# The first stage of a routed cross-attention kernel: biases and condition in one transpose, router's and anchor's products beside the scores, scaling on ScalarE, one difference on GpSimd

## The chip, the cores and the metric

The kernel runs on one core of one Trainium2 chip. The metric is the device time of one execution in microseconds. The profile is taken by the hardware profiler from one more execution of the same program.

## The reference

All arrays are fp32. B = 8 batches, T = 512 tokens, H = 256, RH = 512, E = 3 experts, 64 context rows.

```python
nx = layer_norm(x, ln_gamma, ln_beta)
q, k, v = nx @ Wq, ctx @ Wk, ctx @ Wv
weights = softmax(einsum('bth,bph->btp', q, k) * H ** -0.5)
evidence = einsum('btp,bph->bth', weights, v)
anchor = broadcast(cond[:, None, :])
combined = concat([nx, evidence, anchor], -1)            # 3 H wide
router_probs = softmax(combined @ router_W + router_b)
h = silu(einsum('btc,ecr->bter', combined, e_w1) + e_b1)
expert_out = einsum('bter,erh->bteh', h, e_w2) + e_b2
routed = sum(expert_out * router_probs[..., None], -2)
g = sigmoid(silu(combined @ gate_w1 + gate_b1) @ gate_w2 + gate_b2)
out = x + g * (routed @ out_w + out_b)
```

## The kernel before

The batches are worked in four pairs j = 0 to 3. Features lie on the partitions, tokens along the free axis, so most products are 128 x 128 weights against 512 tokens. Keys are folded into one matrix (`join_keys`, then `project(wkqT, ctxT, keep_m, "m")` gives `mr`), and values are multiplied with the weights beforehand (`value_weights` gives `vw`), so that evidence enters the hidden layers as a product of `vw` with the turned softmax weights `wT`. The products of x with the weights are done in seven instead of eight, Winograd's way: `combine_x` makes differences T (`t1`, `t2`, `t4`) of the four blocks of the scaled x and `t3` in place of a block of `nxT`, and `combine_weights` makes sums `ws` of the weights. `nx_product(j, n, which)` is one of the seven; product 7 reads `t3`, product 3 the block beside it.

The change lies in the work ahead of pair 0 and in the head of its gate layer:

- Loads. SyncE (queue SP) and ScalarE's queue load context, x and the large weights. GpSimd's queue loads the small ones: the biases and the layer norm's vectors into the tile `rows` (28 rows of 128, line 204), the condition into `cond_sb` (8 rows of 256, line 206), `router_W` (line 208) and the router's bias (lines 211, 212). This part of the program is put in order by a scheduler from the dependencies.
- Behind `with tc.manual_schedule(engines=None)` (line 1419) the order on each engine is the order of the program text.
- `small_transposes` (L301) turns `rows` into `cols` (biases, gamma and beta by partition) and the two halves of the condition into `condT`. Its PSUM banks come from `either`, others from `misc`; both hand out banks in turn.
- `statistics`, `deviation`, `normalize` make the normalized rows of x on VectorE with a square root on ScalarE; `transpose_x` (L580) turns them on TensorE, and `scale_x` (L570) scales them out of PSUM, even blocks on VectorE, odd ones on ScalarE.
- `keep_m` (L362) copies the first column of each batch out of PSUM (`m0`) and subtracts it from the others, both on VectorE.
- `router_anchor` (L378) multiplies the condition and beta with the router's columns; `store_router_anchor`, `spread_router_bias` carry its result through DRAM to all partitions on GpSimd's queue.
- `anchor_rows(g)` (L436) multiplies the condition with the anchor part of expert g's or the gate's weights (g = E), 32 columns of weights at a time, four beside each other.
- `scores` (L648), `sum_weights`, `softmax`, `turn_weights` are the attention of pair 0 up to `wT`.
- `gate_layer` (L921) runs the seven products of the gate, with steps of the setup put between by name (`steps.get("gate")`), and ends in `evidence`, which reads `wT` and `vw`.

The order before, as the program text gives it: `small_transposes`, `transpose_x(0)`, `m`, `router_anchor`, `transpose_x(1)`, the gate's `vw`, `scores`, expert 0's `vw`, `anchor_rows(E)`, `anchor_rows(0)`, then the gate layer.

Of the kernel before, what the change touches and what calls it, by code (L numbers as in the profile page):

```python
# [9 lines left out]
AF = mybir.ActivationFunctionType  # L10
# [6 lines left out]
def kernel(  # L17
# [90 lines left out]
    def misc(name):  # L108
        spare.append(spare.pop(0))
        return bank(spare[-1], name)  # L110
# [55 lines left out]
    def by_k(flat, n):  # L166
# [9 lines left out]
    scr = scratch(0, 0, "scr_wa0")  # L176
    wa = {0: by_k(scr[:, :HK], RH), E: by_k(scr[:, HK : HK + KH * H], H)}
    scr = scratch(1, 0, "scr_small")
    zeros, rows, cond_sb = scr[:, :P], scr[:, P : 2 * P], scr[:B, 2 * P : 2 * P + H]
    NL = 2 * P + H  # L180
    rw, rw2, m0, rw_all, gamma_all = (
        scr[:, NL : NL + 3 * KH * E].rearrange("p (k e) -> p k e", e=E),
        scr[:, NL + P : NL + P + KH * TB].rearrange("p (k e) -> p k e", e=TB),
        scr[:, NL + 2 * P : NL + 2 * P + B],
        scr[:, NL + 4 * P : NL + 4 * P + H * E].rearrange("p (d e) -> p d e", e=E),
        scr[:, NL + 4 * P + H * E : NL + 4 * P + H * E + H],
    )
    nc.vector.memset(zeros, 0.0)
    nc.vector.memset(eps_t, LN_EPS)
    nc.vector.memset(warm_t, 1.0)  # L190

    NR = NE + 5 * KH + E * KH
    rows = rows[:NR, :]
    r = 0
    for src, n in (
        (e_b1.rearrange("e (c p) -> (e c) p", p=P), NE),
# [6 lines left out]
    ):  # L203
        nc.gpsimd.dma_start(rows[r : r + n, :], src)
        r += n
    nc.gpsimd.dma_start(cond_sb, cond)
    anchor = slice(2 * H, 3 * H)
    nc.gpsimd.dma_start(rw, rows_of(router_W))
    rb_c = const.tile([ED, 2], F32, tag="rb_c", name="rb_c")
# [77 lines left out]
    def either(name):  # L287
        turn[0] += 1
        return bank((1, 2, 0, 3)[turn[0] % 4], name)
# [10 lines left out]

    def small_transposes():  # L301
        pt = either("pt_rows")
        nc.tensor.transpose(pt[:, :NR], rows, ident[:NR, :NR])
        nc.vector.tensor_copy(cols, pt[:, :NR])
        nc.gpsimd.tensor_copy(b2T[:, :, :E], b2_c.rearrange("p e k -> p k e"))
        pt = either("pt_cond")
        for k in range(KH):
            nc.tensor.transpose(
                pt[:, k * B : (k + 1) * B], cond_sb[:, k * P : (k + 1) * P], ident[:B, :B]
            )  # L310
        nc.vector.tensor_copy(
            condT[:, :, :B], pt[:, : KH * B].rearrange("p (k b) -> p k b", b=B)
        )

    def context_transposes():
# [45 lines left out]

    def keep_m(m, ps):  # L362
        ps = ps.rearrange("p (b c) -> p b c", c=CT)
        nc.vector.tensor_copy(m0, ps[:, :, 0])
        nc.vector.tensor_tensor(
            mr[:, m, :, 1:], ps[:, :, 1:], m0.unsqueeze(2).to_broadcast([P, B, CT - 1]), ALU.subtract
        )


# [6 lines left out]
    rbd = dram.tile([2, NP, ED], F32, tag="rbd", name="rbd")  # L376

    def router_anchor():  # L378
        ps = misc("ps_rb")
        for k in range(KH):  # L380
            nc.tensor.matmul(
                ps[:ED, :B], rwd[:, 2 * KH + k, :], condT[:, k, :B], start=(k == 0), stop=False
            )
        for k in range(KH):

            nc.tensor.matmul(
                ps[:ED, :B], rw2[:, k, :ED], beta_c[:, k : k + 1].to_broadcast([P, B]),
                start=False, stop=(k == KH - 1),
            )
        dst = rrow.rearrange("e (i j) -> e j i", i=2)  # L390
        src = ps[:ED, :B].rearrange("e (j i) -> e j i", i=2)
        nc.scalar.activation(dst, src, AF.Identity, bias=rb_c[:, 0:1])
# [43 lines left out]
    def anchor_rows(g):  # L436


        n = RC if g < E else KH
        ps = misc(f"ps_ar_{g}")[:, : n * QB]  # L440
        for k in range(KH):
            w = wa[g][:, k, :].rearrange("p (c i f) -> p i c f", i=P // QB, f=QB)
            for i in range(P // QB):
                nc.tensor.matmul(  # L444
                    ps[i * QB : (i + 1) * QB, :].rearrange("p (c f) -> p c f", f=QB),
                    condT[:, k, :], w[:, i, :, :], start=(k == 0), stop=(k == KH - 1),
                )
        ar[g] = setup.tile([P, n * QB], F32, tag="ar", name=f"ar_{g}")
        nc.vector.transpose(ar[g], ps)
# [120 lines left out]
    def scale_x(dst, k, src, vector):  # L570
        if vector:
            nc.vector.tensor_scalar(
                dst, src, gamma_c[:, k : k + 1], beta_c[:, k : k + 1], ALU.mult, ALU.add
            )
        else:
            nc.scalar.activation(
                dst, src, AF.Identity, bias=beta_c[:, k : k + 1], scale=gamma_c[:, k : k + 1]
            )

    def transpose_x(b):  # L580
        S["nxT", b] = npool.tile([P, KH, T], F32, tag="nxT", name=f"nxT_{b}")
        for k in range(KH):
            pt = misc(f"pt_x_{b}_{k}")
            for t in range(NT):
                nc.tensor.transpose(  # L585
                    pt[:, t * P : (t + 1) * P], S["xn", b][:, t, k * P : (k + 1) * P], ident
                )
            scale_x(S["nxT", b][:, k, :], k, pt, k % 2 == 0)

    def logits(j):  # L590

# [278 lines left out]
    def keep_part(n, i, d, part):  # L870
        nc.scalar.copy(chunk(n, i, d), part)  # L871
# [49 lines left out]
    def gate_layer(j, steps):  # L921
        n = 0
        for i in range(2):
            for k in range(KH):
                S["hg", i, k] = hpool.tile([P, T], F32, tag=f"hg{i}{k}", name=f"hg_{2 * j + i}_{k}")
        U[n], Z[n], Y[n] = (bank(i, f"ps_{u}_{j}_{n}") for i, u in ((0, "u"), (2, "z"), (3, "y")))
        nx_product(j, n, 1, True)
        keep_part(n, 0, 0, U[n])
        if j == 0:
            anchor_columns(E)  # L930
            anchor_columns(0)
        spares(7, 5)
        nx_product(j, n, 5, True)
        keep_part(n, 1, 1, Z[n])
        nx_product(j, n, 2, True)
        nx_product(j, n, 6)
        keep_part(n, 1, 0, U[n])
        nx_product(j, n, 3)
        for step in steps.get("gate", ()):
            step()  # L940
        nx_product(j, n, 7)
        add(n, 1, 1, U[n])
        for step in steps.get("gate end", ()):
            step()
        if j:
            return
        W = bank(1, f"ps_w_{j}")
        fresh(j, 0)
        evidence(j, [(m, True) for m in PAIRS[0]], W=W)

        add(n, 0, 0, Y[n])
        add(n, 1, 0, Z[n])
        add(n, 1, 1, W)
        silu(j, n, 0, 0)
# [464 lines left out]
    with tc.manual_schedule(engines=None):  # L1419
# [30 lines left out]
        deviation(0, 1)  # L1450
        load_router_column()
        normalize(1)
        load_table(AF.Exp)
        project(wkqT, ctxT, keep_m, "m")
        router_anchor()
        transpose_x(1)
        value_weights(0, E)
        store_router_rows(0)
        store_router_anchor()
        combine_weights(E)  # L1460
        combine_x(0, nc.vector, (0, 1))
        scores(0)
        router_column()
        spread_router_bias()
        combine_weights(0)
        spread_router_rows(0)
        value_weights(0, 0, nc.scalar.copy, False)
        anchor_rows(E)
        anchor_rows(0)
        sum_weights(0)  # L1470
        softmax(0)
        value_differences(0, 0)
        combine_x(0, nc.vector, (2,))
        turn_weights(0)
        late_scratch()
        load_anchor(1)
# [5 lines left out]
        for j in range(NP):  # L1482
# [5 lines left out]
                where.setdefault(n, []).append(lambda: step(*args))  # L1488

            if j == 0:  # L1490
                put(within, "gate", value_weights, 0, 1, nc.scalar.copy, False)
                put(within, "gate", load_table, AF.Silu)
                put(within, (0, "S"), combine_x, 0, nc.vector, (3,))
                put(within, (0, "S"), value_differences, 0, 1)
# [105 lines left out]
```

## Time and profile before

| | |
|---|---|
| median of 3 runs | 459.14 us (458.96 to 460.01) |
| the profiled execution | 458.79 us, of which 456.80 us are the span of the core |
| granted TensorE clock | 1.00 |
| TensorE matmul busy | 451.4 us, 99% of the span |
| VectorE, ScalarE, GpSimd busy | 365.1 us (80%), 213.9 us (47%), 100.2 us (22%) |
| evidence of the first gate begins on TensorE at | 31.33 us |

The span runs from the first to the last instruction of the program; the profiled execution's own time is 2.0 us longer. Times within the span are given in microseconds from its start. Busy time of TensorE is modelled from pipelined matmuls, so gaps between them are read from the start times. PEld is TensorE's weight load, a q behind an engine's name its sequencer.

### The profile page before, as it was taken

The numbers are of one execution on the slowest core, as the hardware profiler recorded it, in microseconds if no ns is written. First come the engines' busy times: TensorE is split into PE (matmuls) and PEld (weight loads), VectorE is DVE, ScalarE is ACT, GpSimd is POOL, SyncE is SP. The second block draws the span as 40 slices with busy tenths as digits, with TensorE's granted clock in tenths as the row PEclk, the third lists the DMA queues.
The fourth block names the chain that finished last, engine by engine and source line by source line (L and its number), as shares of the span: only waits on it lengthen the run. The fifth ranks groups of instructions, "written<-read, shape, count | busy, mean of one in ns | idle before, by whom it ended". The sixth has DMA issues, their size and how long they took to land.

```text
span 456.8 us, 5304 instructions
## 1 busy us (share of the span) xinstructions
PE 451.4 (99%) x1713; PEld 211.5 (46%) x1713; DVE 365.1 (80%) x683; ACT 213.9 (47%) x370; POOL 100.2 (22%) x149
## 2 busy tenths in 40 slices
PE   8999999999999999999999999999999999999997
PEld 6544555444444444444444444444444444444445
DVE  2888979969699999479689999578869846677983
ACT  3445683655221585467220576468220456558000
POOL 6447715001072300001062400001044300000010
PEclk9999999999999999999999999999999999999999
DMA  8975587302011387203011368103011390000014
GB/s 279 371 155 133 97 239 121 93 0 46 7 23 23 56 241 130 83 0 48 6 23 23 48 222 129 20 0 48 6 23 23 50 219 12 0 0 1 0 15 77
DMA packets 119402, 35.30 MB, mean 77 GB/s; under 512 B 106044, under 2 KB 116336, under 8 KB 118864
## 3 DMA queue, kind: packets, MB, share of 16 engines
q1 hardware_dynamic: 115312, 27.02, 29.1%
q0 software_dynamic: 2176, 7.17, 4.8%
q10 hardware_dynamic: 1888, 0.79, 0.6%
q8 instruction: 13, 0.21, 0.2%
q14 instruction: 13, 0.11, 0.1%
HBM read 27.56 MB, written 7.39 MB: 77 GB/s over the span
## 4 chain that ended last, share of the span: by engine, by line
PE 98%; DMA 1%; DVE 0%; SPq 0%; issue 0%
PE ps_u L804 45%; PE ps_z L804 20%; PE ps_y L804 14%; PE ps_vw L777 5%; PE ps_gu L804 3%; PE ps_w2o L505 2%; PE ps_s L655 2%; PE ps_gz L804 2%; PE ps_tokens L804 1%; DMA scr_ctx<-in_ctx_dram 1%; PE ps_v L343 1%; PE ps_m L343 1%; PE ps_gy L804 1%; PE ps_ar L444 0%; PE ps_kq L356 0%; PE pt_x L585 0%
## 5 line engine op out<-in xcount | busy, mean ns | idle before, releaser
L804 PE MATMUL ps_u<-nxT,w 64*128 64x512 f32 (+1 forms) x184 | 86.9, 592 | 0.0
L919 DVE TENSOR_TENSOR h<-h,pb 128x512 f32<-128x512 f32 x96 | 63.4, 697 | 14.9 <-ACT h L862 12.2
L804 PE MATMUL ps_u<-h,w2o 128*128 128x512 f32 x144 | 64.2, 595 | 0.0
L862 ACT ACTIVATE h<-h,abias 128x512 f32<-128x512 f32 x72 | 49.3, 718 | 24.4 <-DVE h L868 24.2
L804 PE MATMUL ps_z<-wT,vw 64*128 64x512 f32 x104 | 51.6, 593 | 0.0
L1324 POOL TENSOR_TENSOR yb<-yb,xb 128x512 f32<-128x512 f32 x14 | 17.7, 1266 | 148.7 <-DVE yb L1323 131.3
L804 PE MATMUL ps_z<-T,ws 64*128 64x512 f32 (+1 forms) x92 | 46.4, 590 | 0.0
L804 PE MATMUL ps_z<-nxT,ws 64*128 64x512 f32 (+1 forms) x92 | 45.9, 590 | 0.0
L804 PE MATMUL ps_y<-nxT,w 64*128 64x512 f32 (+1 forms) x92 | 45.5, 590 | 0.0
L804 PEld LDWEIGHTS ps_u<-nxT,w 64*128 64x128 f32 (+1 forms) x184 | 33.1, 188 | 26.7 <-issue 24.2
L804 PE MATMUL ps_u<-T,ws 64*128 64x512 f32 (+1 forms) x92 | 42.8, 590 | 0.0
L804 PE MATMUL ps_z<-h,w2s 128*128 128x512 f32 x96 | 42.5, 592 | 0.0
L804 PE MATMUL ps_u<-T,w 64*128 64x512 f32 (+1 forms) x98 | 42.4, 590 | 0.0
L804 PEld LDWEIGHTS ps_u<-h,w2o 128*128 128x128 f32 x144 | 27.0, 190 | 32.6 <-issue 30.4
L871 ACT COPY h<-ps_u 128x512 f32<-128x512 f32 x48 | 27.9, 581 | 24.3 <-PE ps_u L804 22.3
L419 POOL DMA_DIRECT2D vrd<-vw x8 | 5.0, 628 | 134.6 <-ACT vw L784 134.6
L1291 DVE TENSOR_TENSOR h<-h,h 128x1024 f32<-128x1024 f32 x24 | 34.3, 1485 | 0.0
L804 PEld LDWEIGHTS ps_z<-h,w2s 128*128 128x128 f32 x96 | 18.2, 190 | 23.0 <-issue 22.3
L804 PE MATMUL ps_y<-wT,vw 64*128 64x512 f32 x56 | 28.0, 596 | 0.0
L804 PE MATMUL ps_u<-wT,vw 64*128 64x512 f32 x56 | 27.9, 595 | 0.0
L777 PE MATMUL ps_vw<-w,vT 128*128 128x512 f32 (+1 forms) x64 | 26.9, 542 | 0.0
L868 DVE TENSOR_TENSOR h<-h,ps_u 128x512 f32<-128x512 f32 x24 | 16.1, 684 | 11.2 <-PE ps_u L804 11.1
(229 smaller groups left out, 811.9 us busy)
## 6 DMA issues: line engine op xcount, KB each, us to landing
pb<-pd POOLq DMA_DIRECT2D x4, 1536.0 KB, 6.5
xb<-in_x_dram SPq DMA_DIRECT2D x64, 64.0 KB, 2.5
out_dram<-yb SPq DMA_DIRECT2D x56, 64.0 KB, 2.0
w<-in_L_xcond_e_w_dram SPq DMA_DIRECT2D x6, 512.0 KB, 10.5
x<-in_x_dram SPq DMA_DIRECT2D x24, 128.0 KB, 3.1
xd<-x SPq DMA_DIRECT2D x24, 128.0 KB, 2.4
xg<-xd SPq DMA_DIRECT2D x48, 64.0 KB, 2.4
scr_wa<-in_L_xcond_e_w_dram SPq DMA_DIRECT2D x3, 512.0 KB, 16.7
```

The lines of the kernel that those rows point to most:

```text
L343: nc.tensor.matmul(ps, w_sb[:, k, m * P : (m + 1) * P], src[:, k, :], start=(k == 0), stop=(k == KH - 1))
L419: nc.gpsimd.dma_start(S["vrd", j][i].rearrange("e c -> c e"), S["vw", j][row_half(i), R0:])
L505: nc.tensor.matmul(ps[:, d * H : (d + 1) * H], w2T[:, k, (i + d) * P : (i + d + 1) * P], ow_sb[:, k, :], start=(k == 0), stop=(k == KH - 1),)
L655: nc.tensor.matmul(ps[side(i, h), g * NH : (g + 1) * NH], mr[:, k, 2 * j + i, g * TB : (g + 1) * TB], S["nxT", 2 * j + i][:, k, h * NH : ( ...
L777: nc.tensor.matmul(ps, vT[:, k, j * 2 * CT : (j + 1) * 2 * CT], w1[:, KH + k, n0:n1], start=(k == 0), stop=(k == KH - 1),)
L804: return nc.tensor.matmul(ps, lhsT, rhs, start=start, stop=True, skip_group_check=not start)
L862: nc.scalar.activation(h, h if src is None else src, AF.Silu, bias=abias[:, c, 2 * j + i : 2 * j + i + 1])
L868: nc.vector.tensor_tensor(h, h, part, ALU.add)
L871: nc.scalar.copy(chunk(n, i, d), part)
L919: nc.vector.tensor_tensor(h, h, S["pb", j][:, i, :, 2 * q // RC, :], ALU.mult)
L1291: nc.vector.tensor_tensor(d, p, m, ALU.subtract)
L1324: nc.gpsimd.tensor_tensor(yb, yb, S["xb", 2 * j + row][:, i, :], ALU.add)
```

## The change

It does five things. (1) The condition is loaded as two DMAs of 8 rows of 128 behind the 28 rows of `rows`, all 128 rows of that tile are set to zero first, and one 128 x 128 transpose gives both `cols` and `condT`. (2) `router_anchor` and `anchor_rows(E)` move to between the gate's `vw` and `scores`, `anchor_rows(0)` directly behind `scores`, and the loading of the table for Exp behind them. (3) For the first x both blocks are scaled by ScalarE; the `m0` copies go to ScalarE, into a place of their own for each half. (4) `t3` of pair 0 is made by GpSimd directly behind its sums of the gate's weights. (5) Expert 1's `vw` is computed before the gate's product 3 and no longer behind it.

```diff
-    zeros, rows, cond_sb = scr[:, :P], scr[:, P : 2 * P], scr[:B, 2 * P : 2 * P + H]
+    zeros, rows = scr[:, :P], scr[:, P : 2 * P]
...
-        scr[:, NL + 2 * P : NL + 2 * P + B],
+        scr[:, NL + 2 * P : NL + 2 * P + KH * B],
...
-    nc.vector.memset(zeros, 0.0)
+    nc.vector.memset(scr[:, : 2 * P], 0.0)
...
-    rows = rows[:NR, :]
...
-    nc.gpsimd.dma_start(cond_sb, cond)
+    for k in range(KH):
+        nc.gpsimd.dma_start(rows[r : r + B, :], cond[:, k * P : (k + 1) * P])
+        r += B
...
         pt = either("pt_rows")
-        nc.tensor.transpose(pt[:, :NR], rows, ident[:NR, :NR])
+        nc.tensor.transpose(pt[:, :P], rows, ident)
         nc.vector.tensor_copy(cols, pt[:, :NR])
         nc.gpsimd.tensor_copy(b2T[:, :, :E], b2_c.rearrange("p e k -> p k e"))
-        pt = either("pt_cond")
-        for k in range(KH):
-            nc.tensor.transpose(
-                pt[:, k * B : (k + 1) * B], cond_sb[:, k * P : (k + 1) * P], ident[:B, :B]
-            )
         nc.vector.tensor_copy(
-            condT[:, :, :B], pt[:, : KH * B].rearrange("p (k b) -> p k b", b=B)
+            condT[:, :, :B], pt[:, NR : NR + KH * B].rearrange("p (k b) -> p k b", b=B)
         )
...
-        nc.vector.tensor_copy(m0, ps[:, :, 0])
+        first = m0[:, m * B : (m + 1) * B]
+        nc.scalar.copy(first, ps[:, :, 0])
         nc.vector.tensor_tensor(
-            mr[:, m, :, 1:], ps[:, :, 1:], m0.unsqueeze(2).to_broadcast([P, B, CT - 1]), ALU.subtract
+            mr[:, m, :, 1:], ps[:, :, 1:], first.unsqueeze(2).to_broadcast([P, B, CT - 1]), ALU.subtract
         )
...
-        ps = misc("ps_rb")
+        ps = either("ps_rb")
...
-        ps = misc(f"ps_ar_{g}")[:, : n * QB]
+        ps = (either if g == E else misc)(f"ps_ar_{g}")[:, : n * QB]
...
-            scale_x(S["nxT", b][:, k, :], k, pt, k % 2 == 0)
+            scale_x(S["nxT", b][:, k, :], k, pt, b > k)
...
         keep_part(n, 1, 0, U[n])
+        for step in steps.get("gate early", ()):
+            step()
         nx_product(j, n, 3)
...
         normalize(1)
-        load_table(AF.Exp)
         project(wkqT, ctxT, keep_m, "m")
-        router_anchor()
         transpose_x(1)
         value_weights(0, E)
+        router_anchor()
+        anchor_rows(E)
         store_router_rows(0)
         store_router_anchor()
         combine_weights(E)
+        load_table(AF.Exp)
         combine_x(0, nc.vector, (0, 1))
         scores(0)
+        anchor_rows(0)
+        combine_x(0, nc.gpsimd, (2,))
         router_column()
         spread_router_bias()
         combine_weights(0)
         spread_router_rows(0)
         value_weights(0, 0, nc.scalar.copy, False)
-        anchor_rows(E)
-        anchor_rows(0)
         sum_weights(0)
         softmax(0)
         value_differences(0, 0)
-        combine_x(0, nc.vector, (2,))
         turn_weights(0)
...
-                put(within, "gate", value_weights, 0, 1, nc.scalar.copy, False)
+                put(within, "gate early", value_weights, 0, 1, nc.scalar.copy, False)
```

## The prediction

> **What bounds the kernel now.** I read the chain of waits on the page first, then TensorE's timeline over the stage that the change touches, then GpSimd's timeline, the DMA issues and the sequencer's rows.
>
> ```profile
> PE 98%; DMA 1%; DVE 0%; SPq 0%; issue 0%
> ```
>
> TensorE is 98% of the chain that ended last, at a granted clock of 1.00 in every stage. So only three things can move the time: TensorE work, the gaps between its instructions, and what it waits for. The change acts before 32 us; behind that, the instruction streams of all engines keep their order. The stage, on TensorE:
>
> ```profile
> 12.54 0.24 PE L303 MATMUL pt_rows<-ident,scr_small 28*128 28x28 f32 x1
> 12.62 0.26 PE L308 MATMUL pt_cond<-ident,scr_small 8*128 8x8 f32 x2
> 12.81 1.09 PE L585 MATMUL pt_x<-ident,x 128*128 128x128 f32 x8
> 13.74 3.60 PE L343 MATMUL ps_m<-scr_ctx,scr_k 128*128 128x512 f32 x8
> 17.27 0.25 PE L381 MATMUL ps_rb<-condT,rwd 128*2 128x8 f32 x4
> 17.37 0.24 PE L386 MATMUL ps_rb<-cols,scr_small 128*2 128x8 f32 x4
> 17.55 1.09 PE L585 MATMUL pt_x<-ident,x 128*128 128x128 f32 x8
> 18.48 1.03 PE L777 MATMUL ps_vw<-w,vT 128*128 128x258 f32 x4
> 19.69 1.93 PE L655 MATMUL ps_s<-nxT,mr 128*32 128x256 f32 x32 [0.18 <-DVE nxT L572]
> 21.55 1.98 PE L777 MATMUL ps_vw<-w,vT 128*128 128x512 f32 x4
> 23.47 0.87 PE L444 MATMUL ps_ar<-scr_wa,condT 128*32 128x64 f32 x32
> 24.27 0.70 PE L804 MATMUL ps_u<-nxT,w 128*128 128x512 f32 x1
> ```
>
> First column start, second busy time. Only the scores show a wait (0.18 us, for VectorE's scaled x). Taken instruction by instruction the starts show small gaps too. A 512-column fp32 step is 0.429, but 0.52 before the router's products (16.75 to 17.27) and before the anchor's (22.95 to 23.47): about 0.09 at each change from full to narrow weights. Changing back costs 0.10 before and 0.10 behind the first full matmul (24.27 to 24.80 is 0.53).
>
> GpSimd's queue, which loads the rows that L303 and L308 transpose:
>
> ```profile
> 1.29 0.66 POOL L204 DMA_DIRECT2D scr_small<-in_L_xcond_e_b_dram  x1 [0.35 <-issue]
> ...
> 2.28 0.52 POOL L204 DMA_DIRECT2D scr_small<-in_L_xcond_gate_b_dram  x1
> ...
> 5.27 0.51 POOL L206 DMA_DIRECT2D scr_small<-in_cond_dram  x1
> 6.33 0.88 POOL L208 DMA_DIRECT2D scr_small<-in_L_xcond_router_W_dram  x1 [0.55 <-DMA scr_small<-in_L_xcond_e_b_dram]
> ```
>
> Eight DMAs go out back to back; the ninth (router_W) waits until the first has landed, because GpSimd's DMAs use eight completion semaphores in turn. Issue to landing:
>
> ```profile
> scr_small<-in_L_xcond_e_b_dram POOLq DMA_DIRECT2D x1, 6.0 KB, 4.8
> ...
> scr_small<-in_cond_dram POOLq DMA_DIRECT2D x1, 8.0 KB, 6.0
> scr_small<-in_L_xcond_router_W_dram POOLq DMA_DIRECT2D x1, 9.0 KB, 6.4
> ```
>
> So cond lands at 5.27 + 6.0 = 11.3, and TensorE's sequencer passes that wait just then:
>
> ```profile
> L308 PEldq EVENT_SEMAPHORE  x1: 51/51/51, 11.3 to 11.3; - x1
> ```
>
> TensorE comes to these rows at 12.54. The cover is 1.2 us.
>
> **TensorE's work, part by part.** Four stretches, before against after.
> - *Rows to ps_m.* 12.54 to 13.74 is 1.20. The two cond transposes go; the rows' one grows from 28 to 128 columns, one transpose step of 0.11. With eight transposes of x at 0.93 that is about 1.05: gain 0.15.
> - *ps_m to ps_vw.* 13.74 to 18.48 is 4.74. Without the eight router products (0.025 each) and their two changes it is 8 x 0.429 + 8 x 0.109 = 4.31: gain 0.43.
> - *ps_vw to the scores.* 18.48 to 19.69 is 1.21: 0.87 of work, 0.34 of change and wait. Now the router's products (0.09 + 0.20) and the gate's anchor rows (23.47 to 23.72, 0.25, with about 0.15 for changes) stand there: 0.87 + 0.69 = 1.56, loss 0.35. The wait has to be gone for this; see VectorE below.
> - *Scores to the gate's first product.* 19.69 to 24.27 is 4.58. Now scores, expert 0's anchor rows and vw follow each other: 1.75 + 0.35 + 0.20 (change) + 1.82 = 4.12: gain 0.46; the gate's first matmul needs no change behind it: gain 0.10.
>
> Sum: 0.15 + 0.43 - 0.35 + 0.46 + 0.10 = 0.8 us of gain, if nothing is late. The earlier ps_vw for expert 1 only changes place with the gate's product 3: nothing.
>
> **The other engines.** Both scalings of the first x go to ScalarE (0.78 each), also the two m0 copies (0.16 on VectorE); ScalarE sat idle 0.72 and 0.92 around there, and its second Sqrt comes some 0.7 later. VectorE normalizes x_1 accordingly later, still 0.2 before TensorE turns it; then two mr subtractions (0.68) and one scaling (0.80) end 0.1 to 0.4 before the scores, by whose place the moved products have added 0.5 of cover. Were that cover gone it would cost the old 0.2. The softmax chain on VectorE, scores to wT, was 10.65 long (19.69 to 30.34) against 11.64 until TensorE's evidence at 31.33. It loses 0.69 (the third difference) and TensorE loses 0.5 there, so 1.1 of slack stays. The third difference on GpSimd takes 1.26 to 2.25 (the same lines in later pairs); it starts after combine_weights(E), about 3.5 behind the scores' start, and product 7 needs it at 10.3: hidden by 4.5 at least. The router's bias load, gg and combine_weights(0) behind it on GpSimd move by at most that; the first was waiting 5.7 for its DMA, and ws of expert 0, ready at 35.2, is read at 38.5.
>
> What GpSimd's subtraction does to VectorE, this trace bounds by its own neighbours:
>
> ```profile
> L646 DVE TENSOR_TENSOR T<-nxT,T x2: 692/824/955, 20.5 to 34.8; 128x512 f32<-128x512 f32 x2
> ```
>
> The 955 ns one ran beside GpSimd subtractions: 0.26 more, so 0 to 0.5 over two instructions, inside the slack; I take none. The Trainium skill, "SBUF — State Buffer", section "Who interferes with whom", speaks against the move: a VectorE instruction with two SBUF inputs and a GpSimd one that reads block each other for a whole instruction. By that rule wT could come 2.25 later, 1.1 beyond the slack, and the sum would be 1.1 worse; the row shows a quarter of a microsecond.
>
> **The queue.** This is the dear part. The zeroing of VectorE now covers the rows, so the rows' DMAs depend on it and the scheduler puts router_W ahead of all of them; cond becomes two DMAs. In GpSimd's built order cond's halves are the ninth and tenth: the first waits for router_W's landing, the second for e_b1's. And TensorE's one transpose now waits for all nine row DMAs.
> - router_W issues at 1.29 and takes 0.88, or 0.15 more as the first (the first of before took 0.66 against 0.50). With the 0.33 that the mask took, e_b1 issues at 2.50 to 2.66.
> - It lands 4.8 to 5.0 later (its own row, and gate_b's, which was second), at 7.3 to 7.6; GpSimd goes on 0.26 after a landing (6.07 to 6.33). So cond's second half issues at 7.6 to 7.9.
> - Issue to landing at that hour: 5.7 for the two rb_c loads issued at 7.43 and 8.10, 6.0 for cond. Far ends: 4.8 and 6.4. So it lands at 13.3 to 13.9; with the far ends at 12.4 to 14.3. I take 13.6, with rb_c's and cond's rows, the nearest in time and in shape.
>
> TensorE then begins the rows at 13.64 in place of 12.54: 1.1 of new wait. Everything behind it shifts alike, since its followers (columns, scaling, ps_m) are fed by it.
>
> A page prices this otherwise: the Trainium skill, "DMA: Bandwidth & Descriptors", section "Anatomy of one DMA — SWDGE (gpsimd) path", fits about 2.0 us and bytes over 436e3. By it the half would land at about 9.8, no wait would arise and the change would gain 0.9; the rows of this trace are 4.8 to 6.4, and they decide.
>
> **Sum.** 1.1 of wait less 0.8 is +0.3 us. The profiled execution took 458.79 (span 456.80, 2.0 around it), which gives 459.1; the median of the three runs lies 0.35 above the profiled one, so 459.14 + 0.3, rounded up for the untested followers of the wait, is 459.5.
>
> **Rivals.**
> 1. *The rows arrive in time* (the wait does not arise): needs the half landed before 12.5, 4.7 after issue. For it: e_b1 took 4.8. Against it: the ten later loads of that queue took 4.9 to 6.4. The gain is then the 0.8 and a further 0.1 (no idle before the transposes): 458.2. At partial waits it lies between.
> 2. *Slower: router_W's 768 pieces of 12 bytes land late and hold the whole chain.* Place: the first half of cond, which waits for router_W's semaphore. At its own 6.4 it lands at 7.7 and the halves issue at 8.0 and 8.5; landing 5.9 later is 14.4, TensorE waits 1.9, net +1.1, and with the 6.4 row for the half as well +1.6: 460.2 to 460.7. It decides from a landing of router_W after 7.4, since before that e_b1's is later. For it: the longest row. Against it: in that row the queue already had seven others ahead; as the first it has none, and the 4.8 of the first fits better.
> 3. *GpSimd's subtraction holds VectorE* past its slack: +0.3 to +1.1, 459.8 to 460.6, from 1.1 of delay on. The 0.26 row speaks against it.
> 4. *It does not do what it says*: if the scores still wait for VectorE, the loss is 0.2, inside the forecast.
>
> **How the numbers follow.** Forecast (landing 13.1 to 14.1) 0.60; rows in time, wholly or half, 0.14; late router_W 0.21; GpSimd against VectorE 0.05. A measurement of this kernel tells about 0.2%, 0.92 us, from no change: below 458.2 is faster, above 460.06 slower. The forecast's own range, -0.2 to +0.8 beside 459.14, lies within. Rival 1 sits on the lower bound: 0.06 faster, 0.08 same. Rivals 2 and 3 are beyond the upper one in most of their reach: 0.22, with 0.06 more from the forecast's tail, 0.28. That leaves 0.66. The range 458.5 to 460.4 leaves out about 0.08 below and 0.12 above.
>
> **What would show it.** Right: router_W first in GpSimd's timeline, cond's second issue at 7.6 to 7.9 with a wait ahead of it, pt_rows at 13.3 to 13.9 with idle "<- DMA scr_small<-in_cond", pt_rows to scores 6.9 long (7.15 before), scores to ps_u 4.1, no wait of TensorE for nxT or wT. Wrong: pt_rows at 12.5; a wait at the scores, at product 7 or at the evidence; any difference behind 32 us.

## The result

The changed kernel took 459.85 us (median of 20 runs, 459.17 to 462.12) against 459.08 for the kernel before in the same session (20 runs, 458.72 to 460.01). The ratio is 1.0016, 95% interval 1.0009 to 1.0024: 0.8 us slower by the medians, less than the 0.92 us that the prediction took as the least that can be told from no change. The forecast was 459.5, range 458.5 to 460.4.

The profiled execution of the changed kernel is the longest of its 20 runs (462.12, span 460.3). The first of the waits below and the projection behind it are longer in it than usual, so a second profiled execution (459.64, the first experiment) is read beside it.

The chain of waits on the page of the changed kernel, by engine:

```profile
PE 94%; DMA 3%; POOL 1%; issue 1%; DVE 0%; ACT 0%; POOLq 0%
```

TensorE was 98% of that chain before and is 94% now: a DMA has come into it, and GpSimd. The waits of TensorE name the places (microseconds in total, times, the longest):

```profile
PE pt_rows L304 <- DMA scr_small<-in_cond_dram: 2.1, 1, 2.1
...
PE ps_u L801 <- POOL gg L404: 0.7, 1, 0.7
```

The first is the wait that the prediction is built on. The second was not foreseen, and the instruction that it names is not the one that caused it. It stands ahead of the gate's fourth pair of products (ps_u from T and ws, `nx_product(j, n, 6)` in the code), called product 6 here. TensorE's timeline over the changed stage (start, busy time, and in brackets the idle time before with what ended it):

```profile
14.52 0.30 PE L304 MATMUL pt_rows<-ident,scr_small 128*128 128x128 f32 x1 [2.10 <-DMA scr_small<-in_cond_dram]
14.65 1.06 PE L582 MATMUL pt_x<-ident,x 128*128 128x128 f32 x8
15.55 5.30 PE L339 MATMUL ps_m<-scr_ctx,scr_k 128*128 128x512 f32 x8
20.69 1.04 PE L582 MATMUL pt_x<-ident,x 128*128 128x128 f32 x8
21.56 1.04 PE L774 MATMUL ps_vw<-w,vT 128*128 128x258 f32 x4
...
22.93 1.91 PE L652 MATMUL ps_s<-nxT,mr 128*32 128x256 f32 x32
...
27.03 1.02 PE L801 MATMUL ps_u<-nxT,w 128*128 128x512 f32 x2
...
30.44 1.10 PE L801 MATMUL ps_u<-T,ws 128*128 128x512 f32 x2 [0.67 <-POOL gg L404]
```

The rows come at 14.52, before at 12.54. The scores wait for nothing now. From the scores to the gate's first product it is 27.03 - 22.93 = 4.10 (4.58 before). The projection ps_m took 5.30 where it took 3.60 before. The clock that TensorE was granted shows why, in windows of one microsecond of that execution (window, its length, then busy time and number of instructions of TensorE, its weight load, VectorE, ScalarE and GpSimd, then granted clock, DMA share, GB/s):

```profile
15.00:16.00 1.00, 1.00 (x8) 0.75 (x7) 0.93 (x7) 0.53 (x1) 0.31 (x2) 0.90 1.05 387
16.00:17.00 1.00, 1.00 (x2) 0.34 (x1) 0.50 (x3) 1.00 (x3) 0.92 (x2) 0.50 1.05 387
17.00:18.00 1.00, 1.00 (x3) 0.48 (x2) 0.82 (x3) 0.11 (x1) 0.25 (x1) 0.50 1.04 385
18.00:19.00 1.00, 1.00 (x3) 0.48 (x2) 0.74 (x3) 0.04 (x1) 0.00 (x0) 0.50 1.05 387
19.00:20.00 1.00, 1.00 (x3) 0.41 (x3) 0.68 (x1) 0.12 (x1) 0.00 (x0) 0.89 1.05 387
```

GpSimd's queue, and what its DMAs took from issue to landing (KB each, median):

```profile
1.32 1.04 POOL L209 DMA_DIRECT2D scr_small<-in_L_xcond_router_W_dram  x1 [0.38 <-issue]
...
8.71 1.00 POOL L206 DMA_DIRECT2D scr_small<-in_cond_dram  x2 [2.49 <-DMA scr_small<-in_L_xcond_router_W_dram]
```

```profile
scr_small<-in_cond_dram POOLq DMA_DIRECT2D x2, 4.0 KB, 5.1
...
scr_small<-in_L_xcond_router_W_dram POOLq DMA_DIRECT2D x1, 9.0 KB, 7.1
```

router_W's load goes first and lands 7.1 later, at 8.43; cond's halves stand behind that landing, and the second, issued at 9.21, is there at 14.32.

For the second wait, the timelines of VectorE, ScalarE and GpSimd around it:

```profile
25.68 0.46 DVE L663 COPY lg<-w 128x8 f32<-128x8 f32 x1
...
27.04 1.68 DVE L670 TENSOR_TENSOR w<-w,mx 128x512 f32<-128x512 f32 x1
```

```profile
28.75 0.63 ACT L671 ACTIVATE w<-w 128x512 f32<-128x512 f32 x1 [3.99 <-DVE w L670]
29.29 0.57 ACT L781 COPY vw<-ps_vw 128x512 f32<-128x512 f32 x1
29.75 0.59 ACT L868 COPY hg<-ps_u 128x512 f32<-128x512 f32 x1
```

```profile
25.66 0.45 POOL L239 TENSOR_TENSOR ws<-ws,w 128x128 f32<-128x128 f32 x1
...
26.90 1.27 POOL L643 TENSOR_TENSOR nxT<-nxT 128x512 f32<-128x512 f32 x1
28.12 1.07 POOL L403 TENSOR_TENSOR gg<-scr_small 128x256 f32<-128x256 f32 x1
29.27 0.73 POOL L404 TENSOR_TENSOR gg<-gg,scr_small 128x256 f32<-128x256 f32 x1
```

L670 is VectorE's subtraction of the maxima (line 673 before, where it took 0.865). It took 1.68, beside the third difference that now runs on GpSimd from 26.90 to 28.17. ScalarE's exponential waits for it, then come ScalarE's copies of vw and of ps_u. The last ends at 29.75 + 0.59 = 30.34, and product 6, which writes a ps_u again, starts at 30.44. In the kernel before, the same chain was in time; there the subtraction started beside the last 0.31 of a GpSimd instruction (L240):

```profile
23.41 0.41 POOL L240 TENSOR_TENSOR ws<-w,ws 128x128 f32<-128x128 f32 x1
```

```profile
23.51 0.86 DVE L673 TENSOR_TENSOR w<-w,mx 128x512 f32<-128x512 f32 x1
```

```profile
24.41 0.63 ACT L674 ACTIVATE w<-w 128x512 f32<-128x512 f32 x1 [4.48 <-DVE w L673]
...
25.43 0.59 ACT L871 COPY hg<-ps_u 128x512 f32<-128x512 f32 x1
```

```profile
26.95 1.02 PE L804 MATMUL ps_u<-T,ws 128*128 128x512 f32 x2
```

The copy ends at 26.02, and product 6 starts at 26.95 without a wait.

From the first product of the evidence to the end of the span it is 425.4 to 425.5 us in the trace before, in the changed kernel's and in all those of the experiments below. So what the versions differ in lies ahead of that product, in the stage that the change touches and in the time at which TensorE comes to it.

### The profile page after: what moved, and what is told of

It is laid out like the page before. It is cut to its first block, busy times and chain, and to the rows that moved or that the text cites. A ratio compares the mean times of both kernels' runs of the same rounds, so it can differ in the third digit from the quotient of the medians.

```text
span 460.3 us, 5301 instructions
## 1 busy us (share of the span) xinstructions
PE 453.0 (98%) x1711; PEld 212.8 (46%) x1711; DVE 364.7 (79%) x679; ACT 214.6 (47%) x373; POOL 101.9 (22%) x151
## 4 chain that ended last, share of the span: by engine, by line
PE 94%; DMA 3%; POOL 1%; issue 1%; DVE 0%; ACT 0%; POOLq 0%
PE ps_u L801 44%; PE ps_z L801 19%; PE ps_y L801 14%; PE ps_vw L774 5%; PE ps_gu L801 3%; PE ps_w2o L502 2%; DMA scr_small<-in_L_xcond_router_W_dram 2%; PE ps_gz L801 1%; PE ps_s L652 1%; PE ps_tokens L801 1%; DMA scr_small<-in_cond_dram 1%; PE ps_m L339 1%; PE ps_gy L801 1%; PE pt_x L582 0%; POOL nxT L643 0%
```

## The experiments

The theory after the result: the change makes TensorE's stage about 0.9 shorter, and gives that back at two places, the rows (late loads of cond) and product 6 (VectorE held by GpSimd's subtraction). Two parts undone, alone and together, test it. Times of one group of kernels come from one session; the kernel before took 459.53 in the first, 459.62 in the second and 459.11 in the third, so the ratios are what can be compared between groups.

**The changed kernel again.** No edit.

> The changed kernel once more, for a second profile, since the first profiled execution (462.12) was the longest of its runs. Theory (three terms: TensorE waits for the condition's second load, its own work is 0.8 shorter, GpSimd's third difference makes TensorE wait at product 6): 459.85, a wait of 1.0 to 1.5 at pt_rows, 0.3 to 0.7 at product 6, ps_m at full clock in 3.4. Rival (the half clock that the first profile shows in ps_m is in every execution and makes the loss): ps_m again over 4.5 long, clock under 0.998.

Measured: 459.88, ratio 1.0008 (0.9999 to 1.0017).

```profile
13.73 0.30 PE L304 MATMUL pt_rows<-ident,scr_small 128*128 128x128 f32 x1 [0.28 <-PE ps_v L339]
14.75 3.60 PE L339 MATMUL ps_m<-scr_ctx,scr_k 128*128 128x512 f32 x8
...
27.96 1.10 PE L801 MATMUL ps_u<-T,ws 128*128 128x512 f32 x2 [0.69 <-POOL gg L404]
```

Here cond landed at 13.53 and TensorE itself came to the rows at about 13.4, so the wait is 0.3, not the 2.1 of the first profile nor the expected 1.0 to 1.5; the clock stays at 1.0 and the projection takes 3.60. The wait at product 6 is the same 0.7. So the size of the first wait changes from execution to execution. The second does not: it is 0.67 to 0.69 in all eight profiles in which the third difference runs on GpSimd ahead of `gg`. GpSimd's queue in this profile has cond's halves at 7.97 and 8.47, 0.27 behind router_W's landing (7.70):

```profile
7.97 1.00 POOL L206 DMA_DIRECT2D scr_small<-in_cond_dram  x2 [1.74 <-DMA scr_small<-in_L_xcond_router_W_dram]
```

**44 rows transposed, no zeroing of the rows** (the loads keep the order of before).

```
-    nc.vector.memset(scr[:, : 2 * P], 0.0)
+    nc.vector.memset(zeros, 0.0)
-        nc.tensor.transpose(pt[:, :P], rows, ident)
+        nc.tensor.transpose(pt[:, : NR + KH * B], rows[: NR + KH * B, :], ident[: NR + KH * B, : NR + KH * B])
```

> The changed kernel with 44 rows transposed in place of 128 and without zeroing the rest, so that the rows' loads no longer depend on VectorE and router_W goes out behind them. Theory: the condition's second half issues at 6.3 and lands at 12.1 to 12.4, no wait at pt_rows, the wait at product 6 stays: 458.4 to 458.8, about 1.2 under the changed kernel. Rival (the loss comes from the moves to ScalarE and GpSimd, the loads are covered): 459.6 to 459.9.

Measured: 458.78, ratio 0.9987 (0.9978 to 0.9996). cond's second half is issued at 6.27 and lands at 11.77, TensorE comes to the rows at 13.49 without a wait. The 0.69 at product 6 stays, with L670 at 1.683.

```profile
27.81 1.10 PE L801 MATMUL ps_u<-T,ws 128*128 128x512 f32 x2 [0.69 <-POOL gg L404]
```

**The third difference back on VectorE.**

```
-        combine_x(0, nc.gpsimd, (2,))
...
         value_differences(0, 0)
+        combine_x(0, nc.vector, (2,))
         turn_weights(0)
```

> The changed kernel with the third difference back on VectorE, where it was. Theory: VectorE's subtraction of the maximum falls from 1.68 to 0.7 to 0.9, ScalarE's Exp and the copies behind it come earlier, no wait at product 6; the wait for the loads stays: 459.2 to 459.5, 0.3 to 0.7 under the changed kernel. Rival (the slack to the evidence absorbs it): 459.85.

Measured: 459.33, ratio 0.9995 (0.9987 to 1.0004). The wait at the rows is there, the one at product 6 is down to 0.2 (it starts at 27.99 where its predecessors end at 27.79). L670 took 1.03 and not the expected 0.7 to 0.9: it now starts 0.13 behind gg's first instruction on GpSimd (25.10 to 25.72) and is held by that.

```profile
14.41 0.30 PE L304 MATMUL pt_rows<-ident,scr_small 128*128 128x128 f32 x1 [1.08 <-DMA scr_small<-in_cond_dram]
```

**Both.**

> 44 rows without zeroing, and the third difference on VectorE. Theory: both waits gone, what stays is the shorter work of TensorE: 458.1 to 458.4, 0.7 to 1.0 under the kernel before. Rival (TensorE's work is not shorter, the moves only shift it): 459.0 to 459.2.

Measured: 458.60, ratio 0.9978 (0.9969 to 0.9987): the first kernel here that clearly beats the one before, by 1.0 us. VectorE's two instructions in it (L670 starts here beside the last 0.20 of a GpSimd instruction, and ahead of gg's):

```profile
23.07 0.17 DVE L663 COPY lg<-w 128x8 f32<-128x8 f32 x1
...
24.14 0.76 DVE L670 TENSOR_TENSOR w<-w,mx 128x512 f32<-128x512 f32 x1
```

The four ratios make a table that nearly adds up: 0.9978 with neither, 0.9987 with GpSimd's subtraction, 0.9995 with the late loads, 1.0008 with both. That is 0.4 us and 0.8 us alone (each with about 0.6 of uncertainty), and 1.4 together. The traces give the stage in single executions: from the start of the last ps_v matmul to the first product of the evidence TensorE took 19.32 before, 18.38 with neither part, 19.31 with GpSimd's subtraction, 19.72 with the late loads, 19.57 in the changed kernel's second profile. By these the subtraction costs 0.93, more than its time says, and the late loads 0.3 to 1.3, by how late TensorE itself is. So both parts cost time, and their sizes are known to half a microsecond.

**Both, and the products of router and anchors back in their old places.**

```
+        router_anchor()
         transpose_x(1)
         value_weights(0, E)
-        router_anchor()
-        anchor_rows(E)
...
         scores(0)
-        anchor_rows(0)
...
         value_weights(0, 0, nc.scalar.copy, False)
+        anchor_rows(E)
+        anchor_rows(0)
```

> Taken from the kernel with 44 transposed rows and the third difference on VectorE (858.. not shown; it measured 458.6, ratio 0.9978): the router's products go back ahead of the first transposes of x_1, both anchors' rows behind the second value weights, the Exp table load ahead of the projection. Theory (the prediction's stretches): the new places of the products save 0.43 - 0.35 + 0.46 + 0.10 = 0.64 us, so this kernel takes 459.2 and its TensorE time from ps_v to the first evidence product is 19.0 against 18.4. Rival (the places are worth nothing, the saving is the single transpose): 458.6 +- 0.2, TensorE time 18.4 to 18.5. A wait of 0.2 at the scores for VectorE may come back under the theory, since the scores then come 0.5 earlier.

Measured: 458.92, ratio 0.9984 (0.9973 to 0.9994), which the times alone can't tell from the 0.9978. The trace can: from the rows to the evidence 18.45 against 17.86, 0.6 as the theory has it. No wait came back at the scores, against the last sentence of the expectation: they start 0.97 behind the value weights' first matmul, against 1.21 with the wait before. The load of the table for Exp, which the expectation names too, stayed where the changed kernel has it.

**Both, with the first block of the first x scaled on VectorE again, and the copies of m0 back there.** (The expectation speaks of x_1; what the edit moves is the block k = 0 of the x with index 0, line 569 at 15.87 on VectorE.)

```
-            scale_x(S["nxT", b][:, k, :], k, pt, b > k)
+            scale_x(S["nxT", b][:, k, :], k, pt, k % 2 == 0)
-        nc.scalar.copy(first, ps[:, :, 0])
+        nc.vector.tensor_copy(first, ps[:, :, 0])
```

> Same base (458.6): the first scaling of x for x_1 and the copies of m0 go back to VectorE. Theory (the moved products give the scores 0.5 us of cover, so ScalarE's help hides anyway): 458.6 +- 0.2, wait at the scores below 0.1. Rival (ScalarE's scaling is what lets the scores start): VectorE has 0.78 + 2 x 0.16 more ahead of the last nxT, the scores wait 0.2 to 0.9, 458.8 to 459.5.

Measured: 458.64, ratio 0.9979 (0.9970 to 0.9988): no difference in the times. In the trace the scores start 1.70 behind the value weights against 1.37 with ScalarE's help, and rows to evidence is 18.25 against 17.86. TensorE sits idle for 0.14 of that, from the end of the anchor's rows at 20.36 to 20.50; VectorE's last scaled block ends at 20.44. So it is ScalarE's help, with the scaling and the copies together, that frees the scores: it does so in the old order too (the run above), and the moved products alone don't. I had said that they do; the trace speaks for the rival, by 0.4 us, which the times don't resolve.

```profile
19.97 0.39 PE L441 MATMUL ps_ar<-scr_wa,condT 128*32 128x64 f32 x13
20.50 1.93 PE L652 MATMUL ps_s<-nxT,mr 128*32 128x256 f32 x32
```

**The changed kernel with router_W's load behind cond's.**

```
+    nc.vector.memset(scr[:, NL : NL + 3 * KH * E], 0.0)
```

> The changed kernel with the zeroing covering router_W's tile too, so that router_W's load loses its place at the head of GpSimd's queue and goes behind cond's halves. Theory (cond's second half waits for a semaphore in turn, whichever load holds it): the halves then wait for a load of 0.5 KB and for e_b1, cond's second half issues 0.3 to 0.8 earlier than in the changed kernel (7.2 to 7.7), lands at 12.7 to 13.5, wait at pt_rows 0 to 0.6, 459.2 to 459.6. Rival (it is router_W's own slow landing that counts, 7 us with its 12-byte pieces): halves issue at 6.5 to 6.9, land by 12.5, no wait at pt_rows, 458.7 to 459.0. Both leave the 0.7 at product 6.

Measured: 458.98, ratio 0.9991 (0.9982 to 1.0000).

```profile
6.37 0.50 POOL L207 DMA_DIRECT2D scr_small<-in_cond_dram  x1 [0.57 <-DMA rb_c<-in_L_xcond_router_b_dram]
7.80 0.52 POOL L207 DMA_DIRECT2D scr_small<-in_cond_dram  x1 [0.94 <-DMA scr_small<-in_L_xcond_e_b_dram]
```

```profile
13.05 0.30 PE L305 MATMUL pt_rows<-ident,scr_small 128*128 128x128 f32 x1 [0.62 <-PE ps_v L340]
```

Each half now stands behind another landing, and the second is issued at 7.80, 0.7 earlier than in the second profile of the changed kernel (8.47) and 1.4 earlier than in the first. The theory of completions in turn holds: another load at the head, and the ninth and tenth DMA wait all the same. But router_W's own slow landing is part of the price too. The second half lands at 12.85 and TensorE, ready at 12.35, still waits 0.6 in this execution; the 0.68 at product 6 stays. So the trace is the theory's, but the time lies below the theory's 459.2 to 459.6 and in the rival's range.

**cond in four loads.**

```
     for k in range(KH):
-        nc.gpsimd.dma_start(rows[r : r + B, :], cond[:, k * P : (k + 1) * P])
-        r += B
+        for b in range(0, B, B // 2):
+            nc.gpsimd.dma_start(rows[r : r + B // 2, :], cond[b : b + B // 2, k * P : (k + 1) * P])
+            r += B // 2
```

> The changed kernel with cond in four DMAs in place of two: the last one then waits for the fourth completion in the queue. Theory (every DMA beyond the eighth waits for one more landing): it issues 0.8 to 1.5 later than the second half does now (8.8 to 10.5), lands at 14.3 to 15.5, TensorE's wait at pt_rows grows by 0.8 to 1.5, to 1.5 to 2.8; time 460.5 to 461.3. With the clock's theory (an idle of over 2 us halves the granted clock over the next projection) 1 to 1.7 more: 461.5 to 462.8, and the granted clock of the windows behind pt_rows shows 0.5 to 0.65. Rival (landing is set by the busy hardware queues, not by the issue): lands within 0.4 of the changed kernel's, 459.9.

Measured: 461.31, ratio 1.0049 (1.0034 to 1.0064). The last load is issued at 9.98 and lands at 14.96. In the profiled execution TensorE started the rows only at 15.40, because its early matmuls were late as well, so that run shows no wait at the rows; the time is at the upper end of the theory's range. Of its six runs four took 460.73 to 461.33 with a mean granted clock of 0.999 to 1.0, and two took 462.23 and 462.48 with 0.995.

**cond in one load of 16 rows.**

```
-    for k in range(KH):
-        nc.gpsimd.dma_start(rows[r : r + B, :], cond[:, k * P : (k + 1) * P])
-        r += B
+    nc.gpsimd.dma_start(rows[r : r + KH * B, :], cond.rearrange("b (k p) -> (b k) p", p=P))
```

> The changed kernel with cond in one DMA of 16 rows (its columns come in the other order out of the transpose, and the copy undoes that). Theory (each DMA past the eighth waits for one more landing): cond waits for router_W's landing alone, issues at 7.9 to 8.7 and lands at 13.0 to 13.9, 0.4 to 0.5 before the second half of now; the wait at pt_rows shrinks by as much, 459.4 to 459.6, and the 0.7 at product 6 stays. Rival (a DMA of 16 rows lands as much later as the second half did): 459.8 to 459.9.

Measured: 459.60, ratio 1.0007 (0.9999 to 1.0016), which is the changed kernel's 1.0008. It was issued at 8.07 and landed at 13.37, in 5.3; the second half of two landed at 13.53 in the profile that is like it. The 0.4 us of the theory do not show, though times that differ by this much are at the edge of what these runs tell.

**GpSimd's gg later.** 44 rows, the third difference on GpSimd, and a further GpSimd subtraction behind it.

```
         combine_x(0, nc.gpsimd, (2,))
+        nc.gpsimd.tensor_tensor(S["T", 0][:, 2, :], S["nxT", 1][:, 1, :], S["nxT", 0][:, 0, :], ALU.subtract)
```

> The kernel with 44 transposed rows and the third difference on GpSimd (458.78), and one more GpSimd subtraction of two 128x512 SBUF tiles right behind the third difference, so that gg comes 1.2 to 1.3 later; its output goes into a tile that is overwritten later, so nothing reads it. Theory (the third difference holds VectorE's subtraction of the maxima for its whole length, the exponential comes late and with it ScalarE's copies ahead of product 6; the added instruction stands beside VectorE's one-input reduction and transpose, which it does not hold): wait at product 6 stays 0.6 to 0.8, time within 0.3 of 458.8. Rival (the profile's releaser is the cause, gg): wait 1.8 to 2.0, time 459.8 to 460.1.

Measured: 459.03, ratio 0.9996 (0.9988 to 1.0005). TensorE, GpSimd and VectorE:

```profile
27.62 1.10 PE L801 MATMUL ps_u<-T,ws 128*128 128x512 f32 x2 [0.69 <-POOL gg L403]
```

```profile
24.07 1.28 POOL L643 TENSOR_TENSOR nxT<-nxT 128x512 f32<-128x512 f32 x1
25.30 1.73 POOL L1465 TENSOR_TENSOR T<-nxT,nxT 128x512 f32<-128x512 f32 x1
26.99 0.61 POOL L403 TENSOR_TENSOR gg<-scr_small 128x256 f32<-128x256 f32 x1
27.68 1.15 POOL L404 TENSOR_TENSOR gg<-gg,scr_small 128x256 f32<-128x256 f32 x1
```

```profile
24.22 1.68 DVE L670 TENSOR_TENSOR w<-w,mx 128x512 f32<-128x512 f32 x1
```

gg now ends at 28.83, 1.2 after product 6 has started, and the wait is the same 0.69. So gg has nothing to do with it: the profile names what ended last before the start. (That is gg's first instruction here, up to 27.60; in the seven other profiles with this wait it ended 1.2 before product 6.) What TensorE waits for is ScalarE's copy of ps_u, which ended 0.09 to 0.10 before product 6 in each of the eight profiles that show this wait.

The lines show how the two engines take turns. L670 starts at 24.22, 0.15 behind GpSimd's difference, and ends at 25.90, which is 0.55 after that ended (25.35). Then the added GpSimd instruction, ready at 25.30, needs 1.73 where its twin took 1.28: it was held until L670 was done. The one that comes second is held until the other has run to its end.

**The third difference behind gg.**

```
-        combine_x(0, nc.gpsimd, (2,))
         router_column()
+        combine_x(0, nc.gpsimd, (2,))
```

> 44 transposed rows, third difference on GpSimd but behind gg. Theory (whole-instruction hold between two-input VectorE instructions and GpSimd ones): the subtraction of the maxima is back at 0.76 to 0.9 us, the exponential is on time and product 6 waits 0 to 0.2; the third difference, now at about 26.2 to 27.5, meets VectorE's product of w and the reciprocals instead, which grows from 0.69 to 1.2 to 1.6, inside the slack of wT: 458.5 to 458.8. Rival (GpSimd slows everything on VectorE in proportion while it runs): the subtraction 0.9 to 1.1, reductions and transposes beside the third difference 20 to 50% longer, wait at product 6 0.2 to 0.4, 458.8 to 459.1.

Measured: 458.10, ratio 0.9979 (0.9970 to 0.9988), the same as with the difference on VectorE. L670 took 1.03, held by gg's first, shorter instruction (23.71 to 24.32); product 6 starts at 26.60 where its predecessors end at 26.41. VectorE's reduction beside GpSimd's difference took the usual 0.69, so the rival (everything slower in proportion) is out. The product of w and the reciprocals took 0.71 and not 1.2 to 1.6, since only 0.16 of it lay beside the difference.

```profile
23.85 1.03 DVE L670 TENSOR_TENSOR w<-w,mx 128x512 f32<-128x512 f32 x1
```

**cond last in the queue, in four loads.**

```
+    anchor = slice(2 * H, 3 * H)
+    nc.gpsimd.dma_start(rw, rows_of(router_W))
+    for k in range(KH):
+        for b in range(0, B, B // 2):
+            nc.gpsimd.dma_start(rows[r : r + B // 2, :], cond[b : b + B // 2, k * P : (k + 1) * P])
+            r += B // 2
```

(put behind both loads of rb_c, in place of the two halves and of router_W's load ahead of them)

> The changed kernel with cond in four DMAs and those moved behind router_W's load and both of router_b's, to the end of GpSimd's queue. Theory (queue): the last waits for the sixth landing of the queue (10.5 to 11.2), issues at 11.0 to 11.8, lands at 15.8 to 16.8, TensorE waits 2.2 to 4. Theory (clock): an idle of that length halves the granted clock of the projection behind it in most executions, as it did in the profiled execution of the changed kernel (idle 2.3) and perhaps in two of the six runs of four loads (mean clock 0.995): +1.5 to 2.0 on top, mean clock 0.993 to 0.996 in most runs, 462.5 to 465. Rival (the low clock of those executions was chance): clock 0.999 to 1.0 in nearly all, 461.8 to 462.8.

Measured: 463.59, ratio 1.0090 (1.0075 to 1.0105).

```profile
16.03 0.30 PE L305 MATMUL pt_rows<-ident,scr_small 128*128 128x128 f32 x1 [2.89 <-DMA scr_small<-in_cond_dram]
16.17 1.05 PE L583 MATMUL pt_x<-ident,x 128*128 128x128 f32 x8
17.06 5.30 PE L340 MATMUL ps_m<-scr_ctx,scr_k 128*128 128x512 f32 x8
```

```profile
18.00:19.00 1.00, 1.00 (x2) 0.34 (x1) 0.47 (x2) 0.46 (x2) 0.33 (x1) 0.50 1.05 389
19.00:20.00 1.00, 1.00 (x2) 0.34 (x1) 1.00 (x4) 0.00 (x0) 0.00 (x0) 0.50 1.04 383
```

TensorE's idle time is 2.9, and the projection ran for most of its time at half the clock. Four of its five runs took 463.57 to 463.94 with a mean clock of 0.995 or 0.996; the fifth took 462.05 with 1.0. So with this idle time the low clock is the rule, while only one of the 20 executions of the changed kernel's result has it. It costs 1.5 (463.6 against 462.05) to 1.7 us (5.30 against 3.60) in an execution that has it. How long TensorE was idle is known for the profiled executions alone. The last load was issued at 10.67, a little before the 11.0 of the theory, and landed at 15.69.

## Why the prediction was right, and where it was not

The time lies in the range and in the class that the prediction held likeliest. Its steps, one by one:

- **TensorE's work, 0.8 shorter: right.** With no wait left ("both") the stretches are: rows to ps_m 1.11 (44 columns there; 1.02 to 1.03 with 128, against "about 1.05"), ps_m to ps_vw 4.31 ("4.31"), ps_vw to the scores 1.37 ("1.56"), scores to the gate 4.11 ("4.12"), gate to evidence 0.11 shorter ("0.10"). The sum is 0.94. The one term off is the loss before the scores, 0.16 and not 0.35: the bound took 0.15 for changes between weights, and they cost next to nothing there.
- **The scores' wait goes: right, but for half of the reason given.** The prediction rested it on ScalarE's scaling and on 0.5 of cover from the moved products ("Were that cover gone it would cost the old 0.2"). With the products in their old places no wait came back (0.97 from the value weights to the scores), with the scaling and the copies back on VectorE one did (0.14). The cover was not needed.
- **The queue: right in kind, and near in its number by errors that offset each other.** router_W goes first, cond's halves stand behind landings, and TensorE waits at the rows. But the landing that holds the second half was taken to be e_b1's, "4.8 to 5.0 later", with the half issued at 7.6 to 7.9. e_b1 took 5.4 in the second profile and 6.0 in the first, and even so router_W decided, by 0.1 to 0.3, as the second rival has it: it took 6.4 and 7.1, the first half followed it at 7.97 and 8.71, and the second half came right behind at 8.47 and 9.21. Then the halves landed 5.1 after issue and not 5.7 to 6.0, so cond was there at 13.53 and 14.32 against "13.3 to 13.9". Last, TensorE was ready for the rows later than the 12.54 of the one profile that the prediction had: at 12.9 to 13.5 in ten of the twelve profiles of the experiments above, at 12.35 and 15.24 in the other two (the start of the last ps_v matmul and 0.52). Nine of these traces show it waiting ahead of its first ps_v products, for 0.2 to 1.2. That made the wait 0.3 in one profile of the changed kernel and 2.1 in the other, against the 1.1 of the sum. The profile of one execution gave a cover (1.2 us) that was itself not steady.
- The page that fits about 2.0 us for such a DMA (the Trainium skill, "DMA: Bandwidth & Descriptors", section "Anatomy of one DMA — SWDGE (gpsimd) path") is not borne out here: 4.7 to 7.1 for the loads of 9 KB and less in this queue, at the same hour as the large loads of the other queues.
- **What GpSimd's subtraction does to VectorE, "inside the slack; I take none": the step that failed.** It cost 0.7 of idle time at product 6. Two mistakes are in it. First, the row of 0.955 against 0.69 was read as the price of standing beside GpSimd, while it was only the price of a short overlap. In the trace before, that subtraction starts at 34.83, when a GpSimd one (34.60 to 35.24) has 0.41 left, and ends at 35.79, 0.55 behind it. The subtraction of the maxima does the same in all 14 profiles: it ends 0.55 behind the GpSimd instruction that it starts beside, so it takes 0.76 with 0.20 of that left ("both"), 0.865 with 0.31 (before), 1.03 with 0.47 and 1.68 with 1.13. L670 went from 0.865 to 1.68, and with the 8-column copy L663, which met one of the weights' subtractions (0.17 to 0.46), the exponential came 1.1 later behind the scores (28.75 - 22.93 against 24.41 - 19.69). Second, the slack was taken from wT to the evidence (1.1 us, and that was enough: no wait for wT appeared). The way that had less slack goes from the exponential through ScalarE's queue: vw's copy and ps_u's copy stand behind it, and product 6 needs ps_u. Before, that copy ended 0.9 ahead of product 6 (26.02 to 26.95); in "both", where the moved products bring the gate closer to the scores, 0.5 (26.52 to 27.00). Rival 3 had the mechanism and the size, +0.3 to +1.1, but not the place, and was given 5%.
- The rule that spoke against the change (the Trainium skill, "SBUF — State Buffer", section "Who interferes with whom": the shared port pair is "an exclusive lock", and a VectorE instruction with two SBUF inputs contends for it with a GpSimd one that reads SBUF) agrees with all the lines above: the more of GpSimd's instruction was left, the longer VectorE's took, from 0.76 to 1.68. It was the row that was read too mildly, and the rule should have been believed.
- **Nothing else moved.** Behind the evidence the traces run parallel, as said: 425.47 us to the end of the span before, 425.45 in both profiles of the changed kernel.

The sum as it happened, for the median: -0.9 of work, about 0.8 for the late loads and 0.4 (by the times) to 0.9 (by the traces) for product 6, against -0.8 and +1.1 and 0. That is +0.3 to +0.8; 0.8 was measured in the session of the result and 0.35 in the first of the experiments. So the time came out right in part by luck: the wait at the rows was smaller than the sum's 1.1, and a wait that the sum put at nothing made up for it. How large the wait at the rows is in the median, and why TensorE comes to the rows at such different times, stays open, since only profiled executions show it.

## What to carry to other kernels

Before moving an instruction to GpSimd, list every VectorE instruction with two SBUF inputs that may start while it runs, add to each what may be left of GpSimd's instruction when it starts (up to 1.13 here), and follow each through every queue that waits for it, not only the one to the end that you watch. Where GpSimd's queue issues small loads, every one past the eighth waits here for the landing of the one eight places before it (4.7 to 7.1 us after its issue). Changing what goes first moved the issue of cond's second half from 6.27 (44 rows) to 8.47 and 9.21, and cutting its two loads into four moved the last one on to 9.98. When a wait names an engine, check whether that engine could have been late without harm: move it later and see.

## What was not expected of the hardware

- The granted clock of TensorE fell to 0.50 for about 3.4 us (the windows above: three full ones and a fifth of each beside them) after an idle time of 2.9 us in one profiled execution and of 2.1 us in another, and not after one of 1.1 us. Each time eight transposes of about 1 us in all lay between the idle time and the projection that ran slow. Of the kernel with 2.9, four executions of five have the low mean clock. The Trainium skill, "TensorE: Matmul & The Clock Gate", section "Part 1: The HAM clock gate (the "warmup" mystery)", speaks of an idle window of about 3.4 us that runs freely. An idle shorter than that was enough here; whether the transposes count as idle these runs don't show.
- A GpSimd instruction is held by VectorE in the same way: gg's first took 0.61 where it ran free and 1.02 to 1.07 where VectorE was ahead of it.
- An 8-column copy on VectorE, with one input, took 0.46 to 0.48 instead of 0.17 when a GpSimd subtraction of 0.45 started up to 0.03 us before it; in "both" the two started together, the copy took 0.17 and GpSimd's instruction 0.49.
